# The last softmax addition as an accumulating DMA, and the denominators one group later

## The chip, the cores and the metric

The kernel runs on one core of a Trainium2 chip. A core has TensorE (PE, with weight loads PEld), VectorE (DVE), ScalarE (ACT), GpSimd (POOL) and SyncE (SP), which issues DMAs. Each engine works through its own instructions in order, and they meet through semaphores. The metric is device time in microseconds (us), as the median of several runs; smaller is better. A profile is of one execution; its span is the time from the program's first instruction to its last.

## The reference

Everything is float32. The input x has 4 sequences of 1024 tokens with 128 features. The block is a sandwich: half a feed-forward step, an attention step, half a feed-forward step.

```python
x = x + 0.5 * ffn(layernorm(x))      # 8 experts, routed by weights per token
x = x + attn(layernorm(x))           # returns its own input as a residual too
x = x + 0.5 * ffn(layernorm(x))

# attn, 16 heads of 64, latent width 64
h   = layernorm(x) * ln_scale + ln_bias
q   = rope(h @ w_down_q.T  @ w_up_q.T)
k   = rope(h @ w_down_kv.T @ w_up_k.T)
v   =      h @ w_down_kv.T @ w_up_v.T
p   = softmax(q @ k.T / 8)           # 1024 x 1024 for each sequence and head
out = (p @ v) @ w_out.T + x
```

The softmax needs, for every query, the sum of its 1024 exponentials: the denominator. It is this sum that the change touches.

## The kernel before, in words

**Stages.** The first feed-forward step runs from the start to about 220 us, the attention loop from there to about 1490 us, the second feed-forward step to the end. Preparation for later stages (norms, latents, the rope, weights of routing) is cut into small steps and spread between the attention loop's instructions.

**Units, slots, groups.** The attention works on *units*. A unit U is one pair of heads (hh = 0, 1) and half the queries (512) of one sequence; there are 64. It has eight *slots*, one for each block of 128 keys (c = 0 to 7). Four slots make a *group* g, so unit U owns groups 2U and 2U + 1. `run` is one loop over groups 0 to 128, and the order in which it calls things is the order on every engine; nothing is reordered later.

In one group PE does, in this order:

- the scores of four slots (`score`, L781): transposed, keys on partitions, 512 queries wide, three matmuls for each head for the parts of the split numbers and a fourth that subtracts the row maximum (maxr). Between them stand the matmuls of `passA` (L755), which work 15 slots ahead and only serve to find row maxima;
- work of the side lists: in even groups the rope's six matmuls (L647), in odd groups the output projection of an earlier unit (`outp`, L839);
- perhaps a small step of preparation (transposes, L285, L299, L596, L602, L615);
- in even groups, the denominators of the unit that ended (`den`, L816);
- the values of the group before (`values`, L804): the product of exponentials and latents, gathered over a unit's eight blocks in the bank psC.

ACT takes the exponential of each score bank (L785) into a tile p of 128 x 2 x 512, one per slot, of which there are eight. It also copies psC (osb, L806), copies the denominators (dsb, L818), scales the outputs (L849) and makes the rope's rounded copies (hi_r, L672).

DVE takes the maxima of each L755 bank (L756, eight in a group; there are two banks, so a third matmul needs the first maximum done), the rope of even groups (L660 to L664) and, in odd groups, the reciprocal of the denominators (L835) and the addition of the outputs to X (L852, L854).

POOL adds up a unit's exponentials (`accumulate`, L797): acc = p0 + p1, then acc + p2, and so on, seven additions of 128 x 1024 in a unit. acc has two buffers. In 18 units (U = 2, 5, ... 53, by `direct`) the eighth block is left out and goes to TensorE instead. POOL also makes the rope's low halves (L680).

**Denominators.** `den(U)` is called in group 2U + 2. Its matmuls multiply a matrix of ones with acc, four of 256 columns, each into its own 32 partitions of one bank; a block left to TensorE gives four more matmuls on its p. ACT copies the bank to dsb, SP stores four rows to memory (d1), and a group later loads them back turned, with queries on partitions (dT). `outp(U)` begins at the start of group 2U + 5: the reciprocal of dT on DVE, the projection of osb on PE, the scaling on ACT, the addition to X on DVE. For the last unit it is a group later.

**SP's queue**, in the loop's order: loads of Q and K for a coming pair of heads, the stores of the rope (from hi_r and eo), the row of maxima (store, then load to maxr), d1 and dT, and in odd groups the two fetches of C_l, on which the next group's rope matmuls work. Each DMA waits for the one eight places before it.

Of the kernel before, what the change touches and what calls it, by code (L numbers as in the profile page):

```python
# [10 lines left out]
F32 = mybir.dt.float32  # L11
F32R = mybir.dt.float32r
AF = mybir.ActivationFunctionType
ALU = mybir.AluOpType
# [4 lines left out]
B, S, D = 4, 1024, 128  # L19
# [10 lines left out]
NGRP = NSLOT // 4  # L30
# [10 lines left out]

def direct(U):

    return 1 if U % 3 == 2 and U < 56 else 0


class Kernel:
# [741 lines left out]
    def accumulate(self, s):  # L789

        nc = self.nc
        U, c = divmod(s, 8)
        if c == 0:
            self.acc_of[U] = self.accp.tile([128, 2, 512], F32, name="acc")
        elif c < 8 - direct(U):
            acc = self.acc_of[U]
            nc.gpsimd.tensor_tensor(acc, self.p_of[s - 1] if c == 1 else acc, self.p_of[s], ALU.add)  # L797

    def values(self, s):
        nc = self.nc  # L800
        U, c = divmod(s, 8)
        b = U // 16
        for hh in range(2):
            nc.tensor.matmul(self.psC[64 * hh:64 * hh + 64, :], self.ckn[b % 2][:, c, :], self.p_of[s][:, hh, :], start=c == 0, stop=c == 7)  # L804
        if c == 7:
            nc.scalar.copy(self.osb_of.pop(U), self.psC)  # L806

    def den(self, U):

        nc = self.nc  # L810
        osb = self.osb_of[U] = self.op2.tile([128, 512], F32, name="osb")
        pd = self.aux()
        parts = [self.p_of[8 * U + c] for c in range(8 - direct(U), 8)] + [self.acc_of[U]]
        for k, part in enumerate(parts):
            for n in range(4):
                nc.tensor.matmul(pd[32 * n:32 * n + 32, 0:256], self.ones, part[:, n // 2, 256 * (n % 2):256 * (n % 2) + 256], start=k == 0, stop=k == direct(U))  # L816
        dsb = self.op1.tile([128, 256], F32, name="dsb")
        nc.scalar.copy(dsb, pd[:, 0:256])  # L818
        dT = self.ms.tile([128, 8], F32, name="dT")

        d1 = self.dram.tile([4, 256], F32, name=f"d1_{U % 4}")
        nc.sync.dma_start(out=d1, in_=dsb[0:128:32, :])
        last = U == 2 * 8 * B - 1
        self.at(self.group + 1, lambda: nc.sync.dma_start(out=dT, in_=d1.rearrange("(h x) (y p) -> p (h x y)", x=2, p=128)), "mid")
        self.at(self.group + (4 if last else 3), lambda: self.outp(U, osb, dT), "side")

    def outp(self, U, osb, dT):

# [29 lines left out]
    def run(self):  # L858
        nc, tc = self.nc, self.tc
# [98 lines left out]
        def pre2(b):  # L958
            return self.ffn_pre(
                self.prep, (2 * b, 2 * b + 1), lambda blk: self.prep.tile([128, 2, 512], F32R, name="xs2"),  # L960
                self.wts2[:, b].rearrange("p e t -> p t e"),
                lambda blk, x2: self.dma(out=self.x2_scr[b][:, :, 512 * (blk % 2):512 * (blk % 2) + 512], in_=x2), b)

        a, c, e = (NP - 3) % 3, (NP - 2) % 3, (NP - 1) % 3
# [15 lines left out]
        def step(most, vector=True):  # L980


            turns["next"] += 1
            found = []
            for i in range(2):
                k = 1 + (turns["next"] + i) % 2
                while streams[k] and streams[k][0] not in needs:
                    v = next(streams[k][0], self)
                    if v is self:
                        streams[k].pop(0)  # L990
                    else:
                        needs[streams[k][0]] = v or OTHER
                if streams[k] and need(k) <= most:
                    found.append(k)
            found = [k for k in found if vector or need(k) != VECTOR]
            if found:
                k = max(found, key=need)
                gen = streams[k][0]
                kind = need(k)
                v = next(gen, self)  # L1000
                if v is self:
                    streams[k].pop(0)
                else:
                    needs[gen] = v or OTHER
                return kind
            return OTHER
# [4 lines left out]
        def rope(g, place):  # L1011
            for d, stages in ROPE[place].items():
                n, r = divmod(g - d, 2)
                if r == 0 and 0 <= n and n + NROPE < 16 * B:
                    for stage in stages.split():
                        self.rope(n + NROPE, stage)

        for g in range(NGRP + 1):
            s0 = 4 * g
            self.group, self.slot = g, s0  # L1020
            rope(g, "side")
            self.run_later(g, "side")

            def rows(hh):
                maxima = lambda i: self.passA(s0 + AHEAD + i, hh) if s0 + AHEAD + i < NSLOT else None
                for n in range(16):
                    if n in MAXIMA[hh]:
                        yield lambda n=n: maxima(MAXIMA[hh].index(n))  # L1030
                    yield lambda n=n: self.score(s0 + n // 4, hh, n % 4) if g < NGRP else None
                if hh == 1:
                    yield lambda: maxima(3)
                yield from side[hh]
                if hh == 0:
                    yield lambda: maxima(3)

            side = self.halves
            for n, pair in enumerate(zip_longest(rows(0), rows(1))):
                for fn in pair:  # L1040
                    if fn:
                        fn()
                if n == 9:
                    rope(g, "mid")
                    self.run_later(g, "mid")
                    step(OTHER)
            self.halves = [[], []]

            b, i = divmod(s0, 128)
            if i == 16 and 1 <= b < B:  # L1050
                streams[1].append(pre2(b - 1))
            self.nrest = 0

            free = g < 16 or g % 2 == 1 or g >= 2 * (16 * B - NROPE) + 2
            step(PE if free else OTHER, free)
            if g and g % 2 == 0:
                self.den(g // 2 - 1)
            rope(g, "end")
            self.run_later(g, "end")
            if g == 1 or (g < NGRP and g % 4 == 3):  # L1060
                P = g // 4 + 3 if g > 1 else 2
                if P < NP:
                    for n, fn in enumerate(self.loads(P)):
                        self.at(g + 1 + n // 8, fn, ("mid", "end")[n // 4 % 2])
                if P == NP + 1:
                    self.ffn_weights2(self.QT[a], self.KT[a], self.QT[c])
                    self.dma(out=xs[0], in_=self.x2_scr[0])

            rope(g, "cast")
            for s in range(s0 - 4, s0):  # L1070
                if s >= 0:
                    self.values(s)
                if s == s0 - 3:
                    step(VECTOR, free)
        for i in range(2):
            for k in range(2):
                for hl in range(2):
                    c = slice(512 * k, 512 * k + 512)
# [3 lines left out]
        with ExitStack() as ctx:  # L1082
# [3 lines left out]
            last = [self.accp.tile([128, 2, 512], F32R, name="acc") for _ in range(2)]  # L1086
            x_of = lambda blk: last[blk - 6] if blk >= 6 else xs[blk // 2][:, :, 512 * (blk % 2):512 * (blk % 2) + 512]
            g = self.ffn_pre(self.prep, (6, 7), x_of, self.wts2[:, 3].rearrange("p e t -> p t e"), rows=3)
# [65 lines left out]
```

## Time and profile before

| | |
|---|---|
| Time, median of 3 runs | 1653.47 us (1652.03 to 1653.92) |
| Profiled execution, span | 1648.4 us |
| PE busy | 1593.2 us, 97% |
| POOL busy | 1456.0 us, 88% |
| DVE busy | 1317.6 us, 80% |
| ACT busy | 1013.5 us, 61% |
| POOL additions L797 | 366 + 64, 872.6 + 152.4 us, 2.38 us each |
| Denominator matmuls L816 | 0.38 us each by the profile |
| DMA engines, attention loop | 55 to 60% busy, 130 to 150 GB/s |
| Granted TensorE clock | 0.994 in the mean, 1.00 from 300 to 1400 us |

The profiled execution has no time of its own beside its span; the median of the runs lies 5.1 us above that.

Lines of the profile name an engine, a line of the kernel, the operation, what it writes and reads, and a count. Matmuls are pipelined: the time between the starts of two of them tells more than the duration of one. A matmul on part of the array can stand twice, so four matmuls of `den` are "x8". A group begins with the first L781 behind an L804.

### The profile page before, as it was taken

How to read it: one execution, taken by the hardware profiler on the slowest of the kernel's cores; microseconds unless marked ns; L12 is line 12 of the kernel's file. 1: busy time of each engine (PE TensorE's matmuls, PEld its weight loads, DVE VectorE, ACT ScalarE, POOL GpSimd, SP SyncE). 2: the span in 40 equal slices, each digit the busy share in tenths (PEclk: the TensorE clock that was granted, in tenths of full speed). 3: DMA queues.
4: the chain of work that ended last, by engine and by line, in shares of the span. 5: the costliest groups of instructions: out<-in, count | busy, mean ns of one | idle time of the engine just before them, and what ended most of it. 6: DMA issues, size and time to landing. Idle time of an engine off the chain costs nothing.

```text
span 1648.4 us, 31237 instructions
## 1 busy us (share of the span) xinstructions
PE 1593.2 (97%) x11044; PEld 1033.2 (63%) x11044; DVE 1317.6 (80%) x2417; ACT 1013.5 (61%) x2220; POOL 1456.0 (88%) x833
## 2 busy tenths in 40 slices
PE   7998989999999999999999999999999999998998
PEld 5876765566566665666565666666566655656776
DVE  6556668888988888888899889889988868616897
ACT  4675666666666666666666656666566655654555
POOL 5668889999999989999999999999999999895676
PEclk9999999999999999999999999999999999999999
DMA  7025557555555655555555556666655532114443
GB/s 226 1 65 166 155 141 168 142 142 130 134 140 140 142 142 134 146 140 138 131 138 142 129 143 152 150 147 141 141 140 149 130 66 53 36 57 138 140 133 103
DMA packets 241149, 212.28 MB, mean 129 GB/s; under 512 B 157664, under 2 KB 170592, under 8 KB 240224
## 3 DMA queue, kind: packets, MB, share of 16 engines
q1 hardware_dynamic: 240992, 210.28, 50.6%
q8 instruction: 87, 1.43, 0.4%
q14 instruction: 70, 0.57, 0.1%
HBM read 130.39 MB, written 79.82 MB: 128 GB/s over the span
## 4 chain that ended last, share of the span: by engine, by line
PE 68%; POOL 3%; DVE 3%; ACT 2%; issue 2%; POOLq 0%; DVEq 0%; ACTq 0%
PE psc L804 24%; PE ps_s L781 21%; PE ps_a L755 6%; PE psx L781 3%; PE ps_s L521 3%; PE ps_s L816 2%; PE psx L476 2%; PE psx L839 2%; POOL acc L797 2%; PE psx L647 2%; ACT p L785 1%; PE ps_s L839 1%; POOL p L529 1%; PE psc L521 1%; DVE m L756 1%
## 5 line engine op out<-in xcount | busy, mean ns | idle before, releaser
L797 POOL TENSOR_TENSOR acc<-acc,p 128x1024 f32<-128x1024 f32 x366 | 872.6, 2384 | 56.3 <-ACT p L785 30.8
L756 DVE TENSOR_REDUCE m<-ps_a 128x1 f32<-128x512 f32 x1024 | 684.8, 688 | 158.0 <-PE ps_a L755 136.2
L785 ACT ACTIVATE p<-ps_s 128x512 f32<-128x512 f32 x896 | 478.2, 602 | 230.7 <-PE ps_s L781 197.1
L781 PE MATMUL ps_s<-QT,KT 64*128 64x512 f32 x2688 | 548.3, 397 | 3.1 <-DVE eo L663 3.0
L804 PE MATMUL psc<-p,ckn 128*64 128x512 f32 x2048 | 468.8, 600 | 0.0
L781 PEld LDWEIGHTS ps_s<-QT,KT 64*128 64x128 f32 x2688 | 351.2, 185 | 138.8 <-issue 76.3
L755 PE MATMUL ps_a<-KT,QT 64*128 64x512 f32 x1024 | 417.9, 419 | 5.0 <-DVE m L756 3.5
L804 PEld LDWEIGHTS psc<-p,ckn 128*64 128x64 f32 x2048 | 135.8, 137 | 257.3 <-issue 252.3
L781 PE MATMUL ps_s<-maxr,one_row 64*128 64x512 f32 x896 | 237.0, 391 | 0.0
L755 PEld LDWEIGHTS ps_a<-KT,QT 64*128 64x128 f32 x1024 | 184.5, 184 | 36.4 <-DVE m L756 12.8
L797 POOL TENSOR_TENSOR acc<-p 128x1024 f32<-128x1024 f32 x64 | 152.4, 2381 | 14.2 <-ACT p L785 11.9
L806 ACT COPY osb<-psc 128x512 f32<-128x512 f32 x64 | 37.6, 587 | 193.3 <-PE psc L804 193.3
L680 POOL TENSOR_TENSOR eo<-eo,hi_r 128x1024 fp32r<-128x1024 f32 x55 | 132.0, 2400 | 0.0
L781 PEld LDWEIGHTS ps_s<-maxr,one_row 64*128 64x128 f32 x896 | 122.3, 185 | 13.5
L781 PE MATMUL psx<-QT,KT 64*128 64x512 f32 x384 | 110.2, 393 | 0.0
L529 POOL TENSOR_TENSOR p<-eo,p 128x512 fp32r<-128x512 f32 x42 | 62.7, 1499 | 40.6 <-ACT p L528 33.1
L425 POOL TENSOR_TENSOR X<-X,dtmp 128x512 f32<-128x512 f32 x54 | 69.1, 1280 | 32.1 <-ACT dtmp L424 31.0
L852 DVE SCALAR_TENSOR_TENSOR X<-ps_s,rT,X 128x128 f32<-128x128 f32 x248 | 68.8, 339 | 26.4 <-PE ps_s L839 26.4
L849 ACT ACTIVATE psx<-psx,rT 128x128 f32<-128x128 f32 x248 | 85.4, 344 | 6.0
L672 ACT CAST hi_r<-eo 128x512 fp32r<-128x512 f32 x128 | 72.9, 615 | 18.8 <-POOL eo L667 14.0
L785 ACT ACTIVATE p<-psx 128x512 f32<-128x512 f32 x128 | 76.9, 601 | 4.4 <-issue 2.1
L781 PEld LDWEIGHTS psx<-QT,KT 64*128 64x128 f32 x384 | 71.1, 185 | 8.5
(237 smaller groups left out, 2388.2 us busy)
## 6 DMA issues: line engine op xcount, KB each, us to landing
C_l<-cs SPq DMA_DIRECT2D x128, 256.0 KB
QT<-qs SPq DMA_DIRECT2D x256, 128.0 KB
KT<-ks SPq DMA_DIRECT2D x256, 128.0 KB
qs<-hi_r SPq DMA_DIRECT2D x32, 512.0 KB
qs<-eo SPq DMA_DIRECT2D x32, 512.0 KB
ks<-hi_r SPq DMA_DIRECT2D x32, 512.0 KB
ks<-eo SPq DMA_DIRECT2D x32, 512.0 KB
rt<-wt SPq DMA_DIRECT2D x52, 256.0 KB
```

The lines of the kernel that those rows point to most:

```text
L425: nc.gpsimd.tensor_tensor(X[:, t:t + 4, :], X[:, t:t + 4, :], tmp, ALU.add)
L529: (nc.gpsimd if m < N - 1 else nc.vector).tensor_tensor(sh[:, 1, :], hp, self.f(sh[:, 0, :]), ALU.subtract)
L672: nc.scalar.copy(w["hi"][:, k, :], w["eo"][:, k, :])
L680: nc.gpsimd.tensor_tensor(w["eo"].bitcast(F32R), w["eo"], self.f(w["hi"]), ALU.subtract)
L755: nc.tensor.matmul(self.psA[hh], self.QT[P % 3][r, 0, q0:q0 + 128], self.KT[P % 3][r, 0, kk * 512:kk * 512 + 512], start=True, stop=True)
L756: nc.vector.tensor_reduce(m[0][:, hh, qb, kk:kk + 1], self.psA[hh], AX.X, ALU.max)
L781: nc.tensor.matmul(ps, w, x, start=k == 0, stop=k == 3)
L785: nc.scalar.activation(self.p_of[s][:, hh, :], ps, AF.Exp, scale=0.125)
L797: nc.gpsimd.tensor_tensor(acc, self.p_of[s - 1] if c == 1 else acc, self.p_of[s], ALU.add)
L804: nc.tensor.matmul(self.psC[64 * hh:64 * hh + 64, :], self.ckn[b % 2][:, c, :], self.p_of[s][:, hh, :], start=c == 0, stop=c == 7)
L849: nc.scalar.activation(po[0][:, c], po[0][:, c], AF.Identity, scale=rT[:, i:i + 1])
L852: nc.vector.scalar_tensor_tensor(x, po[1][:, i * 128:(i + 1) * 128], rT[:, 4 + i:5 + i], x, ALU.mult, ALU.add)
```

## The change

- `direct`: no unit but the last leaves blocks to TensorE; the last one (U = 63) leaves three.
- `accumulate`: in the other 63 units the eighth block is added by a DMA that POOL's queue issues: it reads p (512 KB) and adds it to acc in place. It waits for the exponential and for the addition before it.
- The loop calls `den(U)` in the odd group 2U + 3 instead of 2U + 2, and the last unit's in group 128 as before. On PE the denominators then stand behind the output projection of an odd group, on ACT the copy dsb stands ahead of the scaling L849, and on SP the store d1 stands ahead of the fetches of C_l. `outp` keeps its group, 2U + 5.
- The tile osb is taken when psC is copied, and looked up when `outp` begins.

New waits come with it: the exponential that reuses the eighth block's p, the unit after the next that reuses acc, and the denominators wait for the DMA.

```diff
 def direct(U):
-    return 1 if U % 3 == 2 and U < 56 else 0
+    return 3 if U == 2 * 8 * B - 1 else 0
@@ accumulate
         if c == 0:
             self.acc_of[U] = self.accp.tile([128, 2, 512], F32, name="acc")
+        elif c == 7 and not direct(U):
+            nc.gpsimd.dma_start(out=self.acc_of[U], in_=self.p_of[s], accum_op=ALU.add)
         elif c < 8 - direct(U):
             acc = self.acc_of[U]
             nc.gpsimd.tensor_tensor(acc, self.p_of[s - 1] if c == 1 else acc, self.p_of[s], ALU.add)
@@ values
         if c == 7:
-            nc.scalar.copy(self.osb_of.pop(U), self.psC)
+            osb = self.osb_of[U] = self.op2.tile([128, 512], F32, name="osb")
+            nc.scalar.copy(osb, self.psC)
@@ den
-        osb = self.osb_of[U] = self.op2.tile([128, 512], F32, name="osb")
...
-                nc.tensor.matmul(..., start=k == 0, stop=k == direct(U))
+                nc.tensor.matmul(..., start=k == 0, stop=k == len(parts) - 1)
...
-        self.at(self.group + (4 if last else 3), lambda: self.outp(U, osb, dT), "side")
+        self.at(self.group + (4 if last else 2), lambda: self.outp(U, self.osb_of.pop(U), dT), "side")
@@ run
-            if g and g % 2 == 0:
-                self.den(g // 2 - 1)
+            if g >= 3 and g % 2 or g == NGRP:
+                self.den((g - 2) // 2)
```

More of the change, by code (lines that the diff above doesn't have):

```diff
@@ L815, in den @@
             for n in range(4):
-                nc.tensor.matmul(pd[32 * n:32 * n + 32, 0:256], self.ones, part[:, n // 2, 256 * (n % 2):256 * (n % 2) + 256], start=k == 0, stop=k == direct(U))
+                nc.tensor.matmul(pd[32 * n:32 * n + 32, 0:256], self.ones, part[:, n // 2, 256 * (n % 2):256 * (n % 2) + 256], start=k == 0, stop=k == len(parts) - 1)
         dsb = self.op1.tile([128, 256], F32, name="dsb")
```

## The prediction

> **What bounds the kernel now.** I read the page's busy times first, then the busy time in windows of 100 us, then who waited for the softmax additions, and last the instructions in order of time around the end of single groups. A group is 4 slots of the attention loop; an odd and an even group make one unit.
>
> ```profile
> PE 1593.2 (97%) x11044; PEld 1033.2 (63%) x11044; DVE 1317.6 (80%) x2417; ACT 1013.5 (61%) x2220; POOL 1456.0 (88%) x833
> ```
>
> The windows from 300 to 1300 us show PE busy 98.7 to 100 us in every 100, so in the attention loop PE's instruction stream sets the pace, and POOL (93 to 97) is close behind. The next view tells whether POOL ever stops PE: it lists who waited for the additions of line 797.
>
> ```profile
>   ACT p L785: 25.4, 9
>   PEld ps_s L816: 6.8, 1
>   PE ps_s L816: 5.9, 1
> ```
>
> PE waited once, at the last unit, and its load and its matmul count the same 5.9 us. ACT waited nine times, and where I followed it (from 622.20 and 1098.38) the wait ended before PE needed the result. So a shorter POOL chain buys nothing before the last unit.
>
> Now PE around the denominators (L816). Group 42 (a unit with one block on TensorE) and group 44 (a unit without):
>
> ```profile
> 644.87 0.39 PE L647 MATMUL ps_s<-C_l,wup 64*128 64x512 f32 x1
> 645.20 0.64 PE L816 MATMUL ps_s<-p,ones 128*32 128x256 f32 x8
> 645.66 0.61 PE L816 MATMUL ps_s<-acc,ones 128*32 128x256 f32 x8
> 646.21 3.65 PE L804 MATMUL psc<-p,ckn 128*64 128x512 f32 x16
> ...
> 664.31 0.39 PE L647 MATMUL ps_s<-C_l,wup 64*128 64x512 f32 x1
> 664.64 0.64 PE L816 MATMUL ps_s<-acc,ones 128*32 128x256 f32 x8
> 665.21 3.65 PE L804 MATMUL psc<-p,ckn 128*64 128x512 f32 x16
> 668.79 0.50 PE L781 MATMUL ps_s<-QT,KT 64*128 64x512 f32 x1
> ```
>
> A plain denominator takes PE from 664.64 to 665.21, 0.57 us. With a block on TensorE it is 645.20 to 646.21, 1.01 us, so the second set of four matmuls costs 0.44 (0.42 as the difference of whole groups: 10.10 and 9.68 to 9.70 us). The odd groups, which have no denominator, take 9.30.
>
> DVE at the same place, end of even group 44, start of odd group 45 at 668.79:
>
> ```profile
> 664.06 1.35 DVE L756 TENSOR_REDUCE m<-ps_a 128x1 f32<-128x512 f32 x2 [0.26 <-PE ps_a L755]
> 665.33 1.21 DVE L660 TENSOR_TENSOR rt<-psx,table 128x1024 f32<-128x1024 f32 x1
> ...
> 668.64 0.68 DVE L664 TENSOR_TENSOR eo<-psx,rt 128x512 f32<-128x512 f32 x1
> 669.24 0.19 DVE L835 RECIPROCAL rT<-dT 128x8 f32<-128x8 f32 x1
> 669.36 4.16 DVE L756 TENSOR_REDUCE m<-ps_a 128x1 f32<-128x512 f32 x6
> ```
>
> This is what I build on. In an even group DVE has eight maxima and the rope (L660 to L664), and works almost without a break from its first maximum, 0.57 us into the group, to 669.32. That is 0.53 us into the next, odd group, where its first maximum would start 0.57 in anyway (669.36). It fits with nothing to spare. The rope does not wait for the denominators: it starts behind the eighth maximum, whose matmul stands ahead of them in PE's order.
>
> What a late first maximum costs shows in group 62, where L355 held DVE:
>
> ```profile
> 839.84 1.98 DVE L355 TENSOR_TENSOR g<-ex,below 128x512 f32<-128x512 f32 x1
> 841.74 1.27 DVE L756 TENSOR_REDUCE m<-ps_a 128x1 f32<-128x512 f32 x2
> ```
> ```profile
> 840.53 0.49 PE L781 MATMUL ps_s<-QT,KT 64*128 64x512 f32 x1
> ...
> 842.47 0.50 PE L755 MATMUL ps_a<-KT,QT 64*128 64x512 f32 x1
> ...
> 850.76 0.49 PE L781 MATMUL ps_s<-QT,KT 64*128 64x512 f32 x1
> ```
>
> The first maximum came 1.21 us in, 0.64 late. The third matmul of L755, which needs that bank, came 1.94 in instead of 1.50. The group took 10.23 instead of 9.70: a delay of x costs PE about x - 0.10.
>
> **The change, part by part.**
>
> *Four matmuls gone in 18 units* (U = 2, 5, ... 53): 18 x 0.42 = 7.6 us of PE's stream. PE is the path: **-7.6**.
>
> *Denominators from the even to the odd group.* On PE alone this is nothing: 0.57 less in one group, 0.57 more in the next. But the rope on DVE does not move. An even group shrinks to 9.70 - 0.57 = 9.13 us, and L664 still ends 10.23 after its start (668.64 + 0.68 - 659.09), now 1.10 into the odd group. The reciprocal L835 follows, and the first maximum starts some 0.02 to 0.04 after L664's end (669.36 after 669.32), at 1.12: x = 0.55, a wait of 0.45 on PE in each odd group behind a rope. These are groups 3 to 109, 54 of them: **+24.3**. After it DVE catches up within the odd group (PE leaves 0.9 us between its sixth and seventh maxima), so it doesn't grow. Per unit: 9.13 + 9.30 + 0.57 + 0.45 = 19.45 us, against 19.0 for a unit without a block on TensorE and 19.4 with one.
>
> In an odd group the copy L818 now stands ahead of the four L849 on ACT. PE's denominators start about 5.7 + 0.45 in, L818 follows 0.7 later (664.64, and 606.99 to 607.70), the four L849 end near 8.7, and X (L854) near 9.5, in a group of 10.3; before, it ended some 1.0 ahead of the group's end. I count nothing; the cover is that 0.8 us, and each 0.1 missing costs up to 54 x 0.1 = 5 us.
>
> *Last unit.* Its POOL chain loses three additions of 2.38, 7.2 us, more than the 5.9 that PE waited. It gets 12 matmuls, 3 x 0.42 = 1.3 us. What follows (L804, then the second feed-forward) hangs on PE: **-4.6**.
>
> *POOL.* From 400 to 1300 us it had 305 additions (727 us), 46 of L680 (110) and 22 of small ones; per unit now 6 x 2.38 + 2.40 + 0.47 and some 0.3 between instructions, 17.5 us, and the issue of the DMA. No row shows an issue from POOL. Bounds: 0.32 us, SP's shortest issue, and 2.38, the addition that it replaces. I take 1.2: SP's issues of 0.3 to 0.6 are the nearest rows, but POOL has no hardware queue in this trace, so I go halfway. Up to 19.45 - 17.5 = 1.95 it costs nothing; at 2.38 it costs 0.43 x 62 = 27 us. Queued behind it on POOL are L680, whose place gets no later as long as the issue is under 2.38, and the next unit's additions. [...]
>
> *The transfer's landing* is waited for by the denominators on PE, by the exponential of the next unit's eighth block on ACT (same p buffer), and by the unit after the next on POOL. In unit 19 (groups 38 and 39) four additions ran from 613.89 to 623.68 and the third of them, the seventh block's, ended at about 621.2; the denominators would be at 630.36 + 5.7 = 636.1, the exponential at about 635. So 13 to 14 us are there. The trace has no accumulating transfer. Lower bound 2.5 us: 512 KB at the 211 GB/s of the busiest group (630.36 to 639.69). Upper: the C_l fetch of the same 512 KB, issued by 637.07 and read at 644.19 with no wait, so at most 7.1, times 1.5 for the third pass over the bytes, 10.7. Both fit: 0.
>
> *SP.* The dsb store moves behind the odd group's Q loads and ahead of the C_l fetch, which now waits for L818: its issue ends about 8.6 us into a group of 10.3 and its matmuls (L647) read it 4.5 into the next, 6.2 us later. It needs 2.5 to 7.1 us by the same rows, so 0 to 0.9 late, 0 to 49 us; I take 0, as the 7.1 is only the time until it was read. dT is now loaded about 2 us into an even group, behind K loads, and read (L835) at the next odd one, 7 us later instead of 19; store and load-issue are 2.6 us apart now (609.23 and 611.83), so 0. The row of maxima queued behind dT has a whole group to spare. The tile osb is now taken at its copy instead of a little earlier in the same unit; its buffer was freed by L839 a group before: 0.
>
> *Sum:* -7.6 + 24.3 - 4.6 = +12.1 us on a span of 1648.4, 1660.5. The median of the runs, 1653.47, lies 5.1 above the span; that much stands around it in both kernels: 1653.47 + 12.1 = 1665.6, say **1665**.
>
> [...] By the rows DVE, at 80% of the span, sets 54 groups. [...]
>
> **Rivals.**
> 1. *DVE's overhang costs nothing.* For it: DVE idles 20% of the span, and an odd group's length was 9.30 whether the rope ended 0.1 or 0.5 into it. Against: group 62, and that 0.5 was the edge. Then 1653.5 - 12.2 = **1641**, faster. It decides where the stall per odd group is under 12.2 / 54 = 0.23 us, half of mine.
> 2. *POOL becomes the bound*: an issue of 1.95 us or more. [...] At 2.38 us: 1665 + 27 = **1692**.
> 3. *Transfers come late*: C_l or the accumulation, beside DMA engines that are 55 to 60% busy. Half of the 0.9 us for C_l: 1665 + 24 = **1689**.
>
> **How the numbers follow.** Mine 0.66, rival 1 in full or for the most part 0.13, about balanced (stall near 0.23) 0.07, rivals 2 and 3 together 0.14. My own range is 1658 to 1672 (stall 0.32 to 0.57). The range that holds 8 in 10 cuts most of rival 1 and the far half of 2 and 3: 1648 to 1682. A measurement tells about 0.2%, 3.3 us, from no change: faster 0.13, same 0.07, slower 0.80.
>
> **What the profile after would show.** Right: even groups with a rope near 9.1 us, odd ones near 10.3; waits of L755's weight load on DVE m (L756), 12.8 us in 22 waits before, some 35 us in 70 or more; the denominators with no wait for the DMA; no wait at the last unit; DVE the busier by share, POOL the less. Wrong: odd groups at 9.9 (rival 1), ACT or PE waiting for L797's successors (2), waits of L647 on C_l or of the denominators on the accumulation (3).

## The result, and the profile after

The changed kernel takes 1678.88 us (median of 4 runs, 1675.62 to 1684.21); the kernel before takes 1653.7 us beside it (4 runs). The ratio is 1.0159, 95% interval 1.0134 to 1.0184: slower by some 26 us, where the forecast said 11.5. The direction is the forecast one, the size is more than twice that.

The profiled run of the changed kernel has a span of 1673.8 us against 1648.4, 25.4 more; it is the shortest of the four. Its busy times (part 1 of the page):

```profile
PE 1610.1 (96%) x10924; PEld 1045.3 (62%) x10924; DVE 1306.4 (78%) x2417; ACT 1020.7 (61%) x2220; POOL 1402.5 (84%) x848
```

POOL has lost 53 us of work, DVE 11, and PE 60 matmuls (120 records, since those of `den` stand twice). PE's busy time is 17 us higher all the same, PEld's 12 and ACT's 7, with no instruction more: the ends of matmuls are modelled, and a matmul that is drawn out or slowed counts as busy (in the windows of the last section PE is busy 1.00 of 1.00 us with 3 matmuls from 989.00, at a clock of 0.50, and with 8 from 991.00, at 1.00). So this row does not tell where the time went. I split the span by the starts of the groups' first score matmuls, which can be read in the trace of every run. The loop is here the time from the start of group 0 to the start of group 127, the last.

| | before | after | difference |
|---|---|---|---|
| ahead of the loop | 220.59 | 221.63 | +1.04 |
| loop | 1251.95 | 1281.58 | +29.63 |
| behind it (group 127, last unit's sums, second feed-forward) | 175.88 | 170.64 | -5.24 |

*What went as forecast.* DVE and PE around the start of odd group 41 (first score matmul at 639.99), the changed kernel, instructions in order of time; start, duration, engine, line, operation, and in brackets the idle time ahead of it:

```profile
640.43 0.68 DVE L664 TENSOR_TENSOR eo<-psx,rt 128x512 f32<-128x512 f32 x1
641.02 0.19 DVE L837 RECIPROCAL rT<-dT 128x8 f32<-128x8 f32 x1
641.13 3.90 DVE L756 TENSOR_REDUCE m<-ps_a 128x1 f32<-128x512 f32 x6
```
```profile
640.00 0.49 PE L755 MATMUL ps_a<-KT,QT 64*128 64x512 f32 x1
640.79 0.40 PE L755 MATMUL ps_a<-KT,QT 64*128 64x512 f32 x1
641.83 0.50 PE L755 MATMUL ps_a<-KT,QT 64*128 64x512 f32 x1
```

The rope's last instruction ends 1.1 us into the odd group and DVE's first maximum starts at 1.13 to 1.15 (forecast 1.12). PE's third matmul of L755 starts 1.84 in instead of 1.50. Undisturbed even groups take 9.12 us (forecast 9.13), undisturbed odd ones 10.31 to 10.34 (forecast 10.32). Weight loads of L755 wait 33.7 us in 65 waits (forecast some 35 in 70 or more):

```profile
PEld ps_a L755 <- DVE m L756: 33.7, 65, 1.6
```

*What did not.* The lists of waits of PE and of DVE in the changed kernel (line waiting, what it waited for, us in all, times, longest) have these three rows, and the lists of the kernel before have none for C_l or dT:

```profile
PE psx L647 <- DMA C_l<-cs: 5.4, 2, 3.0
PE ps_s L647 <- DMA C_l<-cs: 4.1, 5, 1.9
```
```profile
DVE rT L837 <- DMA dT<-d: 20.6, 7, 11.0
```

PE waited 9.5 us for the fetch of C_l, in 7 places of six even groups (6, 34, 50, 54, 62 and 74). DVE waited for dT; 15.1 of its 20.6 us fall in groups 125 and 126, the rest in odd groups up to 111, where the eight maxima stand behind the reciprocal. Group 62 shows the first kind, here by SP's queue and by PE (first score matmul at 854.9):

```profile
849.14 2.84 SPq L56 DMA_DIRECT2D KT<-ks  x4
852.02 2.75 SPq L56 DMA_DIRECT2D QT<-qs  x4
854.87 0.57 SPq L824 DMA_DIRECT2D d<-dsb  x1
855.49 1.11 SPq L56 DMA_DIRECT2D C_l<-cs  x2
856.64 3.49 SPq L56 DMA_DIRECT2D KT<-ks  x4
```
```profile
861.96 0.46 PE L647 MATMUL psx<-C_l,wup 64*128 64x512 f32 x1 [2.44 <-DMA C_l<-cs]
```

Eight loads and the denominators' store stand ahead of C_l, so it is issued 0.6 to 1.7 us into the even group, lands at 7.0 and 7.8, and is wanted at 4.7. In group 44, with no loads in the odd group ahead of it, it is issued 2.4 us ahead of the group's start and has landed at 2.0. In the kernel before, the latest of these issues, up to group 108, ended 2.1 us ahead of its group's start.

Groups 86 and 87 (first score matmuls at 1104.88 and 1113.99) show the second kind. dT's load is issued 4.5 us into the even group, and DVE has to wait for it in the odd one:

```profile
1109.40 0.78 SPq L826 DMA_DIRECT2D dT<-d  x1
```
```profile
1116.01 0.20 DVE L837 RECIPROCAL rT<-dT 128x8 f32<-128x8 f32 x1 [0.91 <-DMA dT<-d]
```

### The profile page after: what moved, and what is told of

It is laid out like the page before. It is cut to its first block, busy times and chain, and to the rows that moved or that the text cites. A ratio compares the mean times of both kernels' runs of the same rounds, so it can differ in the third digit from the quotient of the medians.

```text
span 1673.8 us, 31154 instructions
## 1 busy us (share of the span) xinstructions
PE 1610.1 (96%) x10924; PEld 1045.3 (62%) x10924; DVE 1306.4 (78%) x2417; ACT 1020.7 (61%) x2220; POOL 1402.5 (84%) x848
## 3 DMA queue, kind: packets, MB, share of 16 engines
q1 hardware_dynamic: 240992, 210.28, 46.9%
q0 software_dynamic: 9072, 33.03, 10.4%
## 4 chain that ended last, share of the span: by engine, by line
PE 63%; DMA 4%; DVE 3%; ACT 2%; SPq 2%; POOL 2%; issue 1%; POOLq 0%; DVEq 0%; ACTq 0%
PE psc L806 21%; PE ps_s L781 19%; PE ps_a L755 6%; PE psx L781 3%; PE ps_s L521 3%; PE psx L476 2%; DMA C_l<-cs 2%; PE ps_s L818 2%; SPq L56 2%; PE psx L841 2%; DMA dT<-d 2%; PE ps_s L841 1%; DVE m L756 1%; ACT p L785 1%; PE psx L647 1%
## 5 line engine op out<-in xcount | busy, mean ns | idle before, releaser
L799 POOL TENSOR_TENSOR acc<-acc,p 128x1024 f32<-128x1024 f32 x318 | 756.4, 2379 | 73.6 <-ACT p L785 53.3
L756 DVE TENSOR_REDUCE m<-ps_a 128x1 f32<-128x512 f32 x1024 | 675.2, 686 | 174.9 <-PE ps_a L755 148.0
L781 PE MATMUL ps_s<-QT,KT 64*128 64x512 f32 x2688 | 567.9, 399 | 4.6 <-DVE eo L663 3.8
L781 PEld LDWEIGHTS ps_s<-QT,KT 64*128 64x128 f32 x2688 | 356.7, 185 | 138.2 <-issue 60.0
L755 PE MATMUL ps_a<-KT,QT 64*128 64x512 f32 x1024 | 427.5, 428 | 9.4 <-DVE m L756 8.5
L781 PE MATMUL ps_s<-maxr,one_row 64*128 64x512 f32 x896 | 248.2, 392 | 0.1
L755 PEld LDWEIGHTS ps_a<-KT,QT 64*128 64x128 f32 x1024 | 184.6, 184 | 54.6 <-DVE m L756 33.7
L680 POOL TENSOR_TENSOR eo<-eo,hi_r 128x1024 fp32r<-128x1024 f32 x55 | 147.1, 2674 | 1.2 <-ACT hi_r L672 1.2
L781 PEld LDWEIGHTS ps_s<-maxr,one_row 64*128 64x128 f32 x896 | 126.3, 185 | 11.5 <-DMA maxr<-d 0.6
L425 POOL TENSOR_TENSOR X<-X,dtmp 128x512 f32<-128x512 f32 x54 | 69.2, 1281 | 32.0 <-ACT dtmp L424 30.8
L672 ACT CAST hi_r<-eo 128x512 fp32r<-128x512 f32 x128 | 72.8, 614 | 18.7 <-POOL eo L667 14.2
L785 ACT ACTIVATE p<-psx 128x512 f32<-128x512 f32 x128 | 76.9, 601 | 10.2 <-issue 8.4
```

Source lines behind the costliest of these rows:

```text
L425: nc.gpsimd.tensor_tensor(X[:, t:t + 4, :], X[:, t:t + 4, :], tmp, ALU.add)
L672: nc.scalar.copy(w["hi"][:, k, :], w["eo"][:, k, :])
L680: nc.gpsimd.tensor_tensor(w["eo"].bitcast(F32R), w["eo"], self.f(w["hi"]), ALU.subtract)
L755: nc.tensor.matmul(self.psA[hh], self.QT[P % 3][r, 0, q0:q0 + 128], self.KT[P % 3][r, 0, kk * 512:kk * 512 + 512], start=True, stop=True)
L756: nc.vector.tensor_reduce(m[0][:, hh, qb, kk:kk + 1], self.psA[hh], AX.X, ALU.max)
L781: nc.tensor.matmul(ps, w, x, start=k == 0, stop=k == 3)
```

## The experiments

Theory A: the forecast's mechanism holds, and what it lacks are transfers that the change put later on SP's queue. Theory B: it is the added accumulating transfers that make others late, by filling the DMA engines. Theory C: DVE's overhang costs nothing and the loss is all transfers. Differences "against the kernel before" below are ratio times 1652 us, its median in these runs; on that scale the change costs +26.3.

**C_l fetched first.** The fetch is issued ahead of the denominators.

```
             step(PE if free else OTHER, free)
+            rope(g, "end")
             if g >= 3 and g % 2 or g == NGRP:
                 self.den((g - 2) // 2)
-            rope(g, "end")
```

> The changed kernel with one swap: in an odd group the fetch of C_l is issued ahead of the denominators' store (dsb), not behind it. Theory A (the 13 us that the forecast lacks come from transfers that the change put later on SP's queue): PE's waits on C_l, 9.5 us in 7 in the changed kernel, go to 0, and the time falls from 1679 by 9 to 13 us to 1666 to 1670 (ratio to the kernel before 1.008 to 1.010); odd groups behind a rope stay at 10.3 us. Theory B (the fetches are late because the accumulating transfers fill the DMA engines): C_l still lands late in some groups, and the time stays within 4 us of 1679. Theory C (the denominators' place costs only through the transfers, DVE's overhang costs nothing): odd groups fall to 9.9 us and the time to 1645 to 1655.

Measured: 1668.37 us, ratio 1.0096 (1.0081 to 1.0111), +15.9. PE's waits on C_l fell from 9.5 us to 0.5. Odd groups stayed at 10.3, which speaks against C. 10.4 us of the 26.3 are gone with C_l's lateness: A's number, while B expected no more than 4. So the late issue is part of it; this run does not say why the issue is late, and why one that late no longer suffices.

**C_l first and dT's load at the start of the even group.**

```
-        self.at(self.group + 1, lambda: nc.sync.dma_start(out=dT, ...), "mid")
+        self.at(self.group + 1, lambda: nc.sync.dma_start(out=dT, ...), "side")
```

> As the run with C_l fetched first, and the load of dT is issued at the start of the next even group, ahead of its K and Q loads, not in its middle. Theory A: DVE's six waits on dT in the attention groups (9.6 us, without the last unit's) are gone too, the long odd groups 83 and 87 (12.43 and 12.32 us) fall to about 11.3, and the time is 2 to 4 us under that of the first swap alone: 1663 to 1667, the forecast's own sum. Theory B: no change from 1679 beyond 4 us.

Measured: 1666.78 us, ratio 1.0082 (1.0063 to 1.0101), +13.5: no different from the run before it within the intervals. The number lies in A's range, but not for A's reason. In the profile, which is of the longest of the six runs (1671.90), the waits on dT in the loop fell to 0.4 us at most, but PE's waits on C_l came back, 6.8 us in 7:

```profile
PE ps_s L647 <- DMA C_l<-cs: 4.3, 6, 1.6
PE psx L647 <- DMA C_l<-cs: 2.5, 1, 2.5
```

In group 34 C_l was issued 0.3 to 1.5 us into the group, although it stood ahead of the store; with C_l first alone it had been issued 2.3 to 0.4 us before the group's start. SP's whole list ran later there. Moving one transfer forward on a full queue made another late.

**The denominators' move without the accumulating transfer.** The kernel before, with the denominators a group later for the units without a block on TensorE (the lines in `values`, `den` and `outp` that follow from it are left out here).

```
-            if g and g % 2 == 0:
+            if g >= 3 and g % 2 and not direct((g - 3) // 2) or g == NGRP:
+                self.den((g - 2) // 2)
+            elif g and g % 2 == 0 and direct(g // 2 - 1):
                 self.den(g // 2 - 1)
```

> The kernel before, and of the change only this: units with no block on TensorE have their denominators a group later (36 of the 54 behind which a rope runs); all additions stay on POOL, no accumulating transfer, the last unit as before. Theory A: odd groups of these units take 10.3 us and even ones 9.13, 36 x 0.45 = +16 us, and C_l is issued behind the store in these groups, so part of the 10 us of late transfers shows too: 1653.5 + 16 to 25 = 1670 to 1678. Theory B (without the accumulating transfers the fetches are in time): +16 us, 1670, and no wait of PE on C_l. Theory C: odd groups 9.9 us, 1653 to 1660.

Measured: 1667.05 us, ratio 1.0090 (1.0075 to 1.0104), +14.9. Odd groups of the moved units took 10.3 us, the others 9.3; PE's list of waits has no row for C_l. That is B's number (+16, no wait on C_l) and just under A's range (+16 to 25): the move alone, the later place of C_l on SP's queue included, costs the overhang and nothing more.

**The changed kernel without the transfer.** The eighth block is then missing from the sums.

```
         elif c == 7 and not direct(U):
-            nc.gpsimd.dma_start(out=self.acc_of[U], in_=self.p_of[s], accum_op=ALU.add)
+            pass
```

> The changed kernel without the accumulating transfer: the eighth block is left out of the sums (this part of the computation is missing), everything else stays. Theory A (order on SP): PE's waits on C_l stay between 5 and 13 us, POOL's share falls by some 3 points, the time stays at 1672 to 1681. Theory B (the accumulating transfers fill the DMA engines or POOL): the waits on C_l are gone, and the time falls by 9 to 13 us, to 1666 to 1670.

Measured: 1656.62 us, ratio 1.0025 (1.0016 to 1.0034), +4.1. No wait of PE on C_l is left, and none of DVE on dT but two at the last units. Odd groups stayed at 10.3. This is more than either theory expected: the transfer, which nothing waits for, costs 22 us of the 26.3. It rules out A as the whole: the place behind the store makes PE wait for C_l only together with the transfer. Windows of whole groups (44, 45, 46, 47, then 34 and 62) show where it works. First the changed kernel, then the one without the transfer. Behind start, end and length stand the busy times of PE, PEld, DVE, ACT and POOL with their instructions; the last three columns are the granted clock of TensorE, the busy share of the DMA engines (a packet counts where it starts, so it can pass 1), and GB/s:

```profile
670.04:679.14 9.10, 9.10 (x64) 5.76 (x62) 8.00 (x13) 5.28 (x12) 8.35 (x5) 1.00 0.83 198
679.14:689.94 10.80, 10.57 (x82) 6.39 (x80) 8.09 (x16) 8.44 (x20) 9.42 (x5) 1.00 0.61 154
689.94:699.14 9.20, 9.20 (x66) 5.60 (x64) 8.06 (x13) 4.24 (x8) 8.96 (x8) 1.00 0.93 223
699.14:710.24 11.10, 11.10 (x86) 6.78 (x84) 9.42 (x18) 8.17 (x18) 10.54 (x5) 1.00 0.29 78
...
568.14:580.14 12.00, 9.87 (x66) 5.49 (x64) 8.28 (x13) 5.53 (x12) 10.26 (x5) 1.00 0.86 193
...
854.84:867.14 12.30, 9.84 (x64) 5.54 (x62) 8.59 (x14) 4.24 (x8) 10.40 (x5) 1.00 0.88 198
```
```profile
662.64:671.84 9.20, 9.20 (x66) 5.46 (x64) 8.06 (x13) 5.28 (x12) 7.45 (x4) 1.00 0.56 135
671.84:682.64 10.80, 10.59 (x84) 6.41 (x82) 8.03 (x16) 8.45 (x20) 9.75 (x5) 1.00 0.69 174
682.64:691.74 9.10, 9.10 (x64) 5.47 (x62) 8.01 (x13) 4.24 (x8) 8.79 (x8) 1.00 0.61 143
691.74:702.94 11.20, 11.20 (x88) 6.85 (x86) 9.45 (x18) 8.17 (x18) 9.98 (x5) 1.00 0.24 74
...
563.14:572.74 9.60, 9.40 (x64) 5.40 (x62) 8.03 (x13) 5.53 (x12) 7.73 (x4) 1.00 0.64 139
...
845.34:854.44 9.10, 9.10 (x66) 5.62 (x64) 8.30 (x14) 4.24 (x8) 7.84 (x4) 1.00 0.65 145
```

The transfer is issued at the end of the odd group and works in the first 7 us of the even one. It takes these four even groups' DMA share from 0.56 to 0.65 up to 0.83 to 0.93, and in their first 7 us from 0.72 to 0.83 up to 0.96 to 1.06: there the DMA engines are full, and it is in those 7 us that C_l is fetched and dT comes. Part of that room the denominators' move had already taken: in the kernel before, groups 44 and 62 had shares of 0.42 and 0.45. In group 62 C_l is issued at +0.6 and lands at 7.0 and 7.8 with the transfer; without it SP gets to it at -2.4 and it has landed at 2.7. Of these 5.0 us, 2.9 are a later issue and 2.2 a longer way from the end of the issue to the landing (6.0 us against 3.9). dT's load goes the same way: in group 86 it is issued 4.5 us in with the transfer and 2.1 without. SP does not wait for the transfer itself: its list of waits has no row for it. But the loads of Q and K that it issues in even groups land 4.8 us after the end of their issue in the median, against 3.8 to 4.0 without the transfer, and as each DMA of SP waits for the one eight places before, I read the later list as theirs. That step is an estimate: the waits that SP's list puts down to these loads are short (1.1 us on QT and 0.7 on KT in the whole run). The transfer has a queue of its own (33.03 MB, beside 210.28 MB in SP's) and yet slows SP's; how the DMA engines divide their time between the two queues no run shows.

**Half of the transfer.** Half of the eighth block is then missing from the sums.

```
-            nc.gpsimd.dma_start(out=self.acc_of[U], in_=self.p_of[s], accum_op=ALU.add)
+            nc.gpsimd.dma_start(out=self.acc_of[U][:, 0, :], in_=self.p_of[s][:, 0, :], accum_op=ALU.add)
```

> The changed kernel with half of each accumulating transfer (256 of 512 KB; the other half of the eighth block is missing from the sums). The transfer costs 22 us whole and 0 when left out (1678.9 and 1656.6). If the bytes on the DMA engines are what delays the fetches: the waits on C_l fall to under 3 us, and the time is about halfway, 1663 to 1670. If the cost is the transfer itself whatever its size (its issue on POOL, its queue): 1675 to 1680.

Measured: 1658.7 us, ratio 1.0039 (1.0025 to 1.0052), +6.4. PE's waits on C_l are 0.8 us in 2 places. It is the bytes, and neither the issue on POOL (0.88 us in both) nor the number of packets (9072 in both; 16.52 MB instead of 33.03). But the cost is not halfway, as I had expected: half the bytes cost 2.3 us, all of them 22. In the first 7 us of groups 34, 44, 46 and 62 the DMA share is 0.91 to 1.00 here. My reading is that the other transfers have some slack, and that the loss begins when it is used up.

**C_l first and the reciprocal of dT later.** dT is read behind DVE's third maximum, so that a late dT holds no maximum.

```
-        nc.vector.reciprocal(rT, dT)
+        if self.group < NGRP - 1:
+            self.at(self.group, lambda: nc.vector.reciprocal(rT, dT), "mid")
+        else:
+            nc.vector.reciprocal(rT, dT)
```

> The run with C_l fetched first, and in odd groups the reciprocal of dT (L837) stands behind DVE's third maximum, not ahead of the first (the last groups as before). With C_l first, DVE still waited for dT in eight places, and the groups 87, 99 and 107 were 0.5 to 1.1 us longer than without the accumulating transfer. If dT held the maxima, the waits on dT fall to those of the last units, these groups to 11.3, 10.55 and 11.3 us, and the time from 1668 to 1658 to 1663, near the 1656.6 of the run without the transfer. If what is left of the transfer's cost lies elsewhere (QT, KT, the row of maxima): 1666 to 1670.

Measured: 1658.56 us, ratio 1.0041 (1.0025 to 1.0056), +6.8, with the whole transfer in place. DVE's waits on dT are one of 11.6 and one of 8.3 us, both at the last units; groups 87, 99 and 107 lost their excess. The time fell by 9.1 us (15.9 to 6.8, each known to some 2.5 us), but not all of that is dT's lateness: with the reciprocal out of the way undisturbed odd groups take 10.26 us instead of 10.33, some 3 us over 47 groups, which belongs to the overhang. The groups of the profiled runs with and without the transfer tell more: the six even groups in which PE waited for C_l are 14.6 us longer with it, the four odd groups 7, 43, 83 and 87, in which DVE waited for dT, 2.9, and the whole loop 18.6. So the loss sits in these ten groups, most of it with C_l; how it divides when one of the two is mended stays open, since with C_l first dT was late in other groups. The cause is settled from two sides: without the transfer neither is late, and with both made harmless most of what the transfer costs is gone (6.8 against 4.1 without it, or some 6 us left of 22 if the 3 us of overhang are counted).

**Later maxima in the odd groups** (on top of C_l first), against the overhang.

```
-MAXIMA = ((3, 8, 13), (0, 5, 10))
+MAXIMA = (((3, 8, 13), (0, 5, 10)), ((3, 10, 15), (0, 7, 12)))   # even, odd groups
```

> The run with C_l fetched first, and in odd groups the second and third matmul of L755 of either bank stand two rows of score matmuls later in PE's order, so that PE reaches them when DVE is through with the rope. Theory A (the overhang of the rope costs PE a wait in the odd group): odd groups fall from 10.33 to about 9.9 us, and the time falls by 15 to 20 us from 1668 to 1648 to 1653. Rival: DVE's lateness is only pushed to the group's end, where the output rows or the next group's maxima wait for it: odd groups stay at 10.3, and the time at 1664 to 1670.

Measured: 1654.6 us, ratio 1.0012 (0.9994 to 1.0030), +2.0, 13.9 under C_l first alone. Odd groups took 10.04 us instead of 10.33; I had expected 9.9. So the overhang is a real term, and it can be had back by moving PE's matmuls rather than DVE's rope. DVE still waited 27.0 us for dT in 8 places.

**A shorter rope.** One of the rope's five DVE instructions is left out in the changed kernel.

```
-            nc.vector.tensor_tensor(odd, odd, self.table[:, 1, cs], ALU.mult)
```

> The changed kernel without one of the rope's five DVE instructions (the product L662, 0.69 us; the rope's values are wrong then). DVE ends 0.42 us into the odd group in place of 1.10, ahead of the first maximum at 0.57. Theory A: odd groups fall from 10.33 to 9.9 us, 47 to 54 x 0.40, so the time falls by 18 to 21 us from 1679 to 1658 to 1661, with PE's waits on C_l still there. Theory C (the whole loss is late transfers): the time stays within 4 us of 1679.

Measured: 1669.82 us, ratio 1.0113 (1.0085 to 1.0142), +18.7: only 7.6 less than the changed kernel, where 18 to 21 were expected. The mechanism did what was expected: the first maximum starts 0.57 in, the third matmul of L755 at 1.51, and undisturbed odd groups take 9.88. But more than half of the gain was given back. With odd groups 0.45 us shorter, C_l has less time still: behind eight loads its issue ended 0.35 us into the even group in the median, where the changed kernel had 0.27 us ahead of it. PE's waits for it rose from 9.5 to 16.4 us, and DVE's for dT from 20.6 to 30.8. This profile is of the longest of the six runs (1679.24; the shortest took 1664.77), so it shows the way and overstates the amount:

```profile
PE ps_s L647 <- DMA C_l<-cs: 13.1, 9, 2.6
...
PE psx L647 <- DMA C_l<-cs: 3.3, 3, 2.9
```

In five even groups with such a stall TensorE's granted clock also fell, to 0.78 to 0.88 in the mean of the group (34, 62, 74, 90 and 102, windows of whole groups, which take 9.1 to 9.6 us undisturbed):

```profile
562.74:578.04 15.30, 12.83 (x64) 6.38 (x63) 8.60 (x14) 5.52 (x12) 10.39 (x5) 0.78 0.73 158
850.54:864.64 14.10, 11.47 (x64) 5.83 (x62) 9.11 (x15) 4.24 (x8) 10.44 (x6) 0.88 0.77 168
976.74:991.54 14.80, 11.63 (x66) 5.88 (x64) 8.73 (x15) 4.24 (x8) 10.39 (x5) 0.88 0.77 176
1142.44:1156.24 13.80, 11.39 (x64) 6.01 (x62) 8.59 (x14) 4.24 (x8) 12.28 (x9) 0.88 0.77 173
1261.84:1277.54 15.70, 13.00 (x65) 6.39 (x63) 8.59 (x14) 4.52 (x10) 11.67 (x8) 0.78 0.74 149
```

**The last unit alone.** The kernel before, with three blocks of the last unit on TensorE.

```
-    return 1 if U % 3 == 2 and U < 56 else 0
+    return 3 if U == 2 * 8 * B - 1 else 1 if U % 3 == 2 and U < 56 else 0
```

> The kernel before, and of the change only the last unit: three key blocks of unit 63 on TensorE, all else as before. The forecast's tail term: PE's wait of 5.9 us for POOL at the last unit goes, 12 matmuls (1.3 us) come, -4.6 us: 1648 to 1650 (ratio 0.997). Rival: the time after the last unit is set by something else (dT's load, the output rows of attention), then no change, 1653.

Measured: 1645.45 us, ratio 0.9965 (0.9949 to 0.9981), -5.8; the wait for POOL at the last unit is gone from the list. This part of the change is a gain by itself, and this is the fastest kernel of the study.

**All of it mended**: C_l first, later maxima, later reciprocal.

> Later maxima in odd groups, C_l fetched first, and the reciprocal of dT behind the third maximum. By the terms measured so far: 1654.6 with later maxima, less what dT's eight waits of DVE (27.0 us, 11.7 of them at the last units) cost PE, groups 31, 55, 74, 87, 102 by 0.9 to 4 us: 1643 to 1649, faster than the kernel before (ratio 0.995 to 0.999). Rival: as for the run above, 1652 to 1655.

Measured: 1650.21 us, ratio 0.9981 (0.9969 to 0.9993), -3.1, a little over the range expected. It is faster than the kernel before by 0.2%, and still behind the last unit alone: what the change saves on PE in the loop (7.6 us) is about what is left of the overhang (10.04 against 9.88 us in 54 groups, 8.6 us, an estimate) and of late transfers.

## Why the prediction was wrong, point by point

- *What bounds the loop* (PE, with DVE's rope at the edge): right. PE's instructions alone (-7.6 and -4.6, without DVE's overhang, as in rival 1) give 1641, faster, which is wrong in sign: undisturbed odd groups took 10.33 us, and not the 9.88 that they took with the rope shortened.
- *Four matmuls gone in 18 units, -7.6*: right. Even groups of these units fell from 10.11 to 9.12, the 0.42 and the 0.57 of the denominators.
- *Denominators to the odd group, +24.3*: the mechanism and the 0.45 per group were right (10.33 with the whole rope, 9.88 with it shortened). The total was somewhat high: without the transfer the 47 odd groups from 17 to 109 rose by 45.7 us, 26.8 of it denominators (47 x 0.57), which leaves 18.9, 0.40 each. Group 45, for one, rose by 0.74 and not by 1.02, since it had late maxima before.
- *POOL*: right. An issue took 0.88 us (taken: 1.2) and cost no more than some 2.3 us, what the run with half of the transfer, which has the same issue, lost to the one without.
- *The transfer's landing, 0*: right for what it counted. It landed 7.2 us after its issue (4.6 to 10.2; bounds 2.5 to 10.7, where the factor of 1.5 in the upper one was an estimate), and nobody waited for it.
- *Last unit, -4.6*: right; -5.8 alone, and -5.2 behind the loop in the changed kernel.
- **The step that failed** is SP's: "It needs 2.5 to 7.1 us by the same rows, so 0 to 0.9 late, 0 to 49 us; I take 0", and of dT "store and load-issue are 2.6 us apart now (609.23 and 611.83), so 0". Measured, C_l issued first took away 10.4 us and the later reciprocal of dT 9.1 more, some 3 of them overhang; by groups of the profiled runs the two cost 14.6 and 2.9. What failed first is the issue. "its issue ends about 8.6 us into a group of 10.3", 1.7 us ahead of the end, is nearly true of odd groups without loads (1.3 us ahead); with eight loads it ended between 1.3 us ahead and 3.6 us into the next group (74). Without the transfer the same lists end 1.3 us ahead in the median. From the end of its issue to the landing C_l took 3.6 to 6.3 us in the six groups, inside the forecast's 2.5 to 7.1, although these were bounds from the kernel before, whose rows hold no accumulating transfer. dT's load came not 2 us into an even group but 4.5 in the median of those behind eight loads, up to 6.4 (74). I had priced the new transfer by who waits for it, and not by whom it slows: it slows the loads ahead on SP's queue, and so the list behind them. The same text says the DMA engines are 55 to 60% busy, a mean; over the four even groups shown it became 0.83 to 0.93, and in their first 7 us 0.96 to 1.06.
- *The sum*. For the terms without the transfer the forecast was +12.1 on the span, and the profiled run without the transfer has +3.9, 8.2 less; of these, 5.7 are the loop (11.0 measured, 16.7 forecast) and 0.8 the tail, and the rest is the stretch ahead of the loop, 1.7 us shorter in that run. The transfer then added 22 us that stood at 0. The two misses are of opposite sign, so the 13 us between forecast and result understate the second. Rival 3 named this mechanism, and put half of C_l's 0.9 us on every group; it came as waits of up to 3 us in six groups, and through dT besides.

## What to carry to other kernels

A transfer that nobody waits for is not free (here it cost 22 us): price it by the DMA share of the windows that it falls into, and look there for transfers with little slack, above all those that a busy engine waits for. When work is moved between stages, check each engine's place in both, and each queue's longest list and not its usual one. Where a change has parts, the smallest can be the whole gain: here three blocks of the last unit on TensorE, 5.8 us.

## What the runs showed of the hardware

Here a wait of PE of 2.96 us cost more than its length, 5.5 us. Group 74 of the changed kernel, windows from its start to its end; the clock is the third column from the right:

```profile
978.90:983.00 4.10, 4.10 (x36) 3.40 (x36) 3.42 (x7) 2.49 (x5) 3.64 (x3) 1.00 1.01 217
983.00:986.40 3.40, 0.66 (x6) 0.20 (x2) 0.68 (x2) 1.75 (x4) 3.32 (x2) 1.00 1.02 249
986.40:988.00 1.60, 1.09 (x5) 0.69 (x7) 0.69 (x1) 0.00 (x0) 1.52 (x2) 0.83 1.00 234
988.00:989.00 1.00, 1.00 (x5) 0.44 (x3) 0.10 (x1) 0.00 (x0) 1.00 (x1) 0.50 1.03 371
989.00:990.00 1.00, 1.00 (x3) 0.29 (x4) 1.00 (x2) 0.00 (x0) 0.86 (x1) 0.50 0.73 73
990.00:991.00 1.00, 1.00 (x6) 0.33 (x4) 0.90 (x2) 0.00 (x0) 0.00 (x0) 0.57 0.05 1
991.00:992.00 1.00, 1.00 (x8) 0.33 (x6) 1.00 (x2) 0.00 (x0) 0.00 (x0) 1.00 0.00 0
```

```profile
986.62 0.47 PE L647 MATMUL psx<-C_l,wup 64*128 64x512 f32 x1 [2.96 <-DMA C_l<-cs]
```

The DMA engines are full, and PE stands idle for 2.96 us ahead of 986.62 (second fence, PE's instruction there). Then the clock is halved for about 3.4 us (0.83, 0.50, 0.50 and 0.57 in the four windows from 986.40 on, which makes 0.5 us of the third window, 2.0 in the next two, 0.9 in the sixth). The group takes 14.60 us instead of 9.12: 3 us of waiting and the rest slower work and what follows from it. Group 62, with a wait of 2.44, kept its full clock. In the kernel with the shorter rope the waits ahead of the five slow groups' drops were 2.28, 2.47, 2.88, 2.41 and 2.55 us (34, 62, 74, 90, 102), so the length of the wait alone does not decide it. In these six cases the clock fell after 2.28 to 2.96 us without a matmul; what else decides it these rows do not show.

The second surprise is how sharp the cost of the bytes is: half of each transfer 2 us, all of it 22.
